# Two more groups of nodes summed from buckets in a graph network's first layer, and self edges only counted there

## The chip, the cores and the metric

The kernel runs on one core of a Trainium2 chip. A core has TensorE (PE; its weight loads are listed as PEld), VectorE (DVE), ScalarE (ACT), GpSimd (POOL) and SyncE (SP), the last of which only issues DMAs here. The metric is the device time of one execution in microseconds. Times of several executions are given by their median.

## The reference

Two layers of a graph network act on 12500 nodes with 128 features each. There are 212500 edges: 100000 drawn at random, the same ones reversed, and one from every node to itself. The list comes sorted by `dst`.

```python
h = relu(layernorm(x))
# layer 0: message passing and a gated cell
msg = h[src] @ W_msg.T + b_msg + edge_embed[type]        # one row per edge
messages = segment_sum(msg, dst)                         # one row per node
x = x + gru_cell(messages, h, W_ih, W_hh, b_ih, b_hh)
# layer 1
h = relu(layernorm(x))
agg = segment_sum(h[dst], src)                           # 'col' is dst, 'row' is src
y = ((1 + eps) * h + agg) @ W1.T + b1
y = relu(batchnorm(y) * gamma + beta)
x = x + y @ W2.T + b2
```

In layer 0 the sum over edges is taken before the matrix: the kernel sums h[src] and counts the edge types of each node, and the small matrices act on these sums.

## The kernel before, in words

**Preparation (to about 123 us).** The rows h are computed, split into three bfloat16 parts that add up to the float32 value (`PARTS0` = 3, so a row has `W0` = 384 columns) and stored in HBM as `table0`. Every edge is packed into one word.

**Two ways of summing in layer 0.** The nodes below `SPLIT0` are summed by *chunks*: a chunk is 128 neighbouring edges of the sorted list. `gather` (L1218) issues one indirect DMA per chunk on POOL's queue, which fetches the 128 source rows from `table0`; eight chunks share a buffer `g`, and there are three such buffers. `match` (L1226) compares the target nodes with a row of places on DVE, eight chunks at once, and L1324 makes a matrix of edge types in the same way. `add_chunk` (L1239, L1242) multiplies each of the three parts with the match and adds one matmul that counts the types; where a chunk crosses a border of 256 nodes, each of these is cut in two.

The nodes from `SPLIT0` on are summed by *buckets*. The last 7056 nodes form 28 groups of 252 nodes, and the first `FIRST` groups of them go by chunks. A bucket holds the edges from one block of 256 source nodes to one group of targets, at most 128. All of `table0` lies in SBUF for it, as `held`. For each of the `NB` = 49 blocks, `take_rows` (L1377) selects up to 128 rows by two matmuls with a 0/1 matrix `take`, ACT turns the result into bfloat16 `rows` (L1379), and `put_rows` adds them to the group's sums by three matmuls (L1386) with a 0/1 matrix `put`, and to the type counts by a fourth (L1388). `put_rows` runs two buckets behind `take_rows`. `prepare` builds `take`, `put` and `kind` for four buckets (`UNIT`) at a time on DVE (L1358, L1363, L1369) and loads the source numbers `others` on SP's queue (L1354).

Edges from a node to itself have an extra place: with every node having at least one, they would overfill the bucket that holds the node's own block. So each group has three more buckets (`PORTIONS` = 3, `NV` = 52), one for each third of the group's nodes. Before, their rows are taken from `held` as well, at a place that L948 to L961 work out edge by edge when the buckets are sorted (L922 to L928 make the offsets). Their type code is raised by 9, so that the counts of types 9 to 17 are those of self edges.

**The sort.** `make_buckets` sorts the words of each group on DVE by a sorting network (L476), with transposes on TensorE, and writes the lists back; up to about 373 us a step of it follows every chunk. `make_list` sorts the list for layer 1 in the same manner, later, beside the loop. Its end makes a row of numbers on POOL (`starts`, L350), which DVE needs (L351).

**The loop and its order.** One loop runs over the chunks. Once the buckets are made, the loop issues, after each chunk, as many bucket steps and list steps as keep them in proportion to the chunks that are left, so that chunks, buckets and the list end together. While the buckets are made, the order of the instructions on each engine is the one that is written; afterwards it is planned ahead by a scheduler.

**The cell.** When 512 nodes (504 in the bucket stream) are summed, a `cell` is queued: a generator whose steps are issued one after every second chunk. It multiplies the sums and the type counts with the small matrices (L635, L636), reads off how many self edges each node has (L643, `times`, which scales the node's own row in layer 1), turns the node's own rows into columns (`hT`, L653, L656), computes the gates (L661 to L664), the new row (L669 to L688), its layernorm, and stores rows for layer 1. Every one of these steps uses the same PSUM bank, `work`. The sums `own` and the counts `types` may be written again for the next 512 nodes once `sl.consumed` is set.

**Layer 1 (from about 1600 us).** It has chunks (gathers from `front1`) and buckets (`back1`) of its own. Its first bucket loads wait until the space of `held` is free. The groups of `back1` that are written last are loaded late; which these are depends on `FIRST` (`late_`).

Of the kernel before, what the change touches and what calls it, by code (L numbers as in the profile page):

```python
# [38 lines left out]
F32 = mybir.dt.float32  # L39
# [12 lines left out]
P = 128  # L52
# [12 lines left out]
FRACTION = 10  # L65
FIRST = 10
SUB = 256
# [10 lines left out]
def tile_gnn(  # L78
# [45 lines left out]
    PORTION = -(-GROUP // PORTIONS)  # L124
    TOP_TILE = 2 * NB - 2
    assert D == P and EC <= FULL and E <= P * FULL and N < NPAD and E % P
# [194 lines left out]
    for h in range(2):  # L321
# [298 lines left out]

    def cell(sl, own, types, pool, psum, store):

# [4 lines left out]
        def work():  # L627
            return psum.tile([P, SLICE], F32, name="work")
# [3 lines left out]
        xs = load_x(sl, pool)  # L632
        yield
        pm = work()
        nc.tensor.matmul(pm[:, :n], env.w["msg"][:, 0, :], own[:, :n], start=True, stop=False)  # L635
# [12 lines left out]
        sl.consumed = True  # L648
        yield
        tp = work()  # L650
        for k, r_ in tiles:
            for j in range(PARTS0):
                nc.tensor.matmul(tp[:, k * high:k * high + r_], hp[:r_, k, j * D:(j + 1) * D],  # L653
                                 ident16[:r_, :r_], start=j == 0, stop=j == PARTS0 - 1)
        hT = pool.tile([D, SLICE], F32, name="hT")
        nc.scalar.copy(hT[:, :n], tp[:, :n])  # L656
        yield
# [249 lines left out]
    def make_buckets(keys, pool, psum):  # L907
# [13 lines left out]
        for k in range(PORTIONS):  # L921
            nc.vector.tensor_scalar(tile_i[:, k, :], lead, float(k * PORTION), None, op0=OP.add)  # L922
        nc.vector.tensor_single_scalar(tile_i, tile_i, P.bit_length() - 1, op=OP.logical_shift_right)
        nc.vector.tensor_scalar(more, tile_i, float(TOP_TILE), float(-P), op0=OP.min, op1=OP.mult)
        for k in range(PORTIONS - 1, 0, -1):
            nc.vector.tensor_tensor(more[:, k, :], more[:, k, :], more[:, k - 1, :], op=OP.subtract)
        nc.vector.tensor_scalar(more[:, 1:, :], more[:, 1:, :], float(BLOCK), None, op0=OP.add)
        nc.vector.scalar_tensor_tensor(more[:, 0, :], more[:, 0, :], float(NB * BLOCK), lead, op0=OP.add,  # L928
                                       op1=OP.add)
        yield from wait(2)  # L930
# [10 lines left out]
        for c in range(0, HALF, some):  # L941
            h = c // some
            word = raw[:, c:c + some]
            here, over = scratch[:, :some], scratch[:, some:]
            ints = [part.tile([P, some], I32, name=f"ints{k}") for k in range(3)]
# [309 lines left out]
    with tc.tile_pool(name="cell", bufs=1) as pool, tc.tile_pool(  # L1255
# [5 lines left out]
        class Stream:  # L1261
# [83 lines left out]
        def bucket_steps():  # L1345
# [4 lines left out]
            def prepare(g, b0):  # L1350

                others = unit.tile([P, UNIT * P], BF16, name="others")
                a = sources0[g, b0:b0 + UNIT, :]
                nc.sync.dma_start(others, bass.AP(tensor=a.tensor, offset=a.offset,  # L1354
                                                  ap=[[0, P], [1, UNIT * P]]))
                i, j = divmod(b0, QJ)
# [11 lines left out]
                for t in range(2):  # L1368
                    nc.vector.tensor_scalar(take[:, t, :], others, own_row[:, 2 * t:2 * t + 1], None,  # L1369
                                            op0=OP.is_equal)  # L1370
                return take, put, kind

            def take_rows(g, b, take):
                t0 = 2 * b if b < NB else min((SPLIT + g * GROUP + (b - NB) * PORTION) // P, TOP_TILE)
                ps = next(taken_banks)[:, :W0]
                for t in range(2):
                    nc.tensor.matmul(ps, take[:, t, :], held[:, t0 + t, :], start=t == 0, stop=t == 1)  # L1377
# [4 lines left out]
            def put_rows(h, rows_, put, kind):  # L1382
                sums, counts = by_bucket.sums.of(h)
                final = by_bucket.sums.used(h)
                for j in range(PARTS0):
                    nc.tensor.matmul(sums[:, :GROUP], rows_[:, j * D:(j + 1) * D], put, start=False,  # L1386
                                     stop=final and j == PARTS0 - 1, skip_group_check=True)
                nc.tensor.matmul(counts[:, :GROUP], kind, put, start=False, stop=final,  # L1388
                                 skip_group_check=True)
                by_bucket.sums.flush()  # L1390
# [4 lines left out]
            for u, (g, b0) in enumerate(units):  # L1395
                take, put, kind = coming
                for k in range(UNIT):
                    rows_ = take_rows(g, b0 + k, take[:, :, k * P:(k + 1) * P])
                    flying.append((g - FIRST, rows_, put[:, k, :], kind[:, k, :]))
                    if len(flying) > LAG:  # L1400
# [404 lines left out]
```

## Time and profile before

| | us |
|---|---|
| median of the three runs shown | 2594.92 (2593.8 to 2598.58) |
| the profiled execution, its own time | 2603.78 |
| its span, from the first to the last instruction | 2602.0 |
| TensorE busy (modelled) | 2250.3 (86%) |
| weight loads busy | 1896.3 (73%) |
| VectorE busy | 2117.8 (81%) |
| ScalarE busy | 1322.5 (51%) |
| GpSimd busy | 1860.4 (71%) |
| gathers of layer 0 (L1218 from `table0`) | 1064, 1006 ns each |
| count matmuls of buckets (L1388) | 936 |

How to read the rows: a line of a group or of the timeline names the line of the kernel, the engine, the operation, what is written and what is read, the shapes and how often. "MATMUL bank<-put,rows 128*128 128x252" has 128 x 128 weights and 252 columns that pass through them. In the timeline, neighbouring instructions of one kind are merged: the first number is the start of the first, the second the time to the end of the last. A matmul's end is modelled, and matmuls overlap; the distance from one start to the next is what a matmul costs when TensorE is never idle. A float32 matmul appears as two instructions. In the rows of waits, the releaser is the engine whose work came last; "issue" means that nothing was waited for that the profile shows. The granted clock (PEclk) is the share of full speed that TensorE was allowed. Indirect DMAs are POOL's instructions, and their busy time is the time that POOL needs to issue them.

### The profile page before, as it was taken

The numbers are of one execution on the slowest core, as the hardware profiler recorded it, in microseconds if no ns is written. First come the engines' busy times: TensorE is split into PE (matmuls) and PEld (weight loads), VectorE is DVE, ScalarE is ACT, GpSimd is POOL, SyncE is SP. The second block draws the span as 40 slices with busy tenths as digits, with TensorE's granted clock in tenths as the row PEclk, the third lists the DMA queues.
The fourth block names the chain that finished last, engine by engine and source line by source line (L and its number), as shares of the span: only waits on it lengthen the run. The fifth ranks groups of instructions, "written<-read, shape, count | busy, mean of one in ns | idle before, by whom it ended". The sixth has DMA issues, their size and how long they took to land. (4 is left out here: it accounts for less than half of the span.)

```text
span 2602.0 us, 52858 instructions
## 1 busy us (share of the span) xinstructions
PE 2250.3 (86%) x19810; PEld 1896.3 (73%) x19834; DVE 2117.8 (81%) x3899; ACT 1322.5 (51%) x2726; POOL 1860.4 (71%) x1886
## 2 busy tenths in 40 slices
PE   2033469899999999999999797899999999999996
PEld 1023347677677777777777575799999999999995
DVE  8898759896568878788787565699999999999983
ACT  4475125455566655656565364444444444444443
POOL 4876477777777777777777676377777777777770
PEclk9996659999999999999999898899999999999998
DMA  5662234454445444545455356655555555555584
GB/s 155 203 205 67 84 100 128 122 128 127 131 132 143 131 134 127 149 129 132 127 150 131 90 144 187 171 154 156 157 158 159 159 159 156 159 160 160 153 217 128
DMA packets 308267, 374.73 MB, mean 144 GB/s; under 512 B 44815, under 2 KB 263093, under 8 KB 308001
## 3 DMA queue, kind: packets, MB, share of 16 engines
q0 software_dynamic: 85504, 197.27, 28.7%
q1 hardware_dynamic: 217451, 171.44, 23.3%
q8 instruction: 158, 2.59, 0.4%
q10 hardware_dynamic: 5046, 2.55, 0.3%
q14 instruction: 108, 0.88, 0.1%
HBM read 327.18 MB, written 43.91 MB: 143 GB/s over the span
## 5 line engine op out<-in xcount | busy, mean ns | idle before, releaser
L1218 POOL DMA_INDIRECT g<-table,idx x1064 | 1070.9, 1006 | 354.9 <-issue 298.4
L1218 POOL DMA_INDIRECT g<-front,idx x690 | 692.8, 1004 | 258.5 <-issue 189.5
L1239 PE MATMUL bank<-m,g 128*128 128x128 bf16 (+25 forms) x5790 | 687.8, 232 | 101.5 <-DMA g<-table,idx 53.0
L1379 ACT CAST rows<-bank 128x384 bf16<-128x384 f32 x936 | 441.8, 478 | 410.3 <-PE bank L1377 407.6
L1542 ACT CAST rows<-bank 128x512 fp32r<-128x512 f32 x686 | 402.7, 588 | 470.8 <-PE bank L1539 468.3
L1539 PE MATMUL bank<-mine,take 126*128 126x256 f32 x2744 | 475.0, 295 | 16.0 <-issue 11.6
L1377 PE MATMUL bank<-held,take 128*128 128x384 bf16 x1872 | 464.5, 328 | 2.4 <-ACT rows L1379 1.6
L1386 PE MATMUL bank<-put,rows 128*128 128x252 bf16 x2808 | 460.1, 272 | 0.0
L1239 PEld LDWEIGHTS <-g 128*128 128x128 bf16 x3912 | 299.5, 103 | 200.0 <-DMA g<-table,idx 94.5
L1552 PE MATMUL bank<-put,rows 128*128 128x256 f32 x2744 | 443.1, 284 | 2.2 <-DVE put L1527 1.9
L1527 DVE TENSOR_TENSOR put<-places,nodes 128x1024 fp32r<-128x1024 f32 x343 | 412.9, 1213 | 5.4 <-PE bank L1552 5.4
L1358 DVE TENSOR_TENSOR put<-places,nodes 128x1008 bf16<-128x1008 f32 x234 | 281.3, 1202 | 157.0 <-PE bank L1388 156.7
L1539 PEld LDWEIGHTS bank<-mine,take 126*128 126x128 f32 x2744 | 374.2, 191 | 28.0 <-issue 21.8
L1552 PEld LDWEIGHTS bank<-put,rows 128*128 128x128 f32 x2744 | 378.0, 190 | 6.8 <-issue 3.6
L1386 PEld LDWEIGHTS <-rows 128*128 128x128 bf16 x2808 | 274.9, 98 | 130.1 <-issue 4.1
L1522 DVE TENSOR_SCALAR take<-others,own_row 126x512 fp32r<-126x512 bf16 x686 | 302.4, 491 | 64.1 <-PE bank L1539 33.6
L1226 DVE TENSOR_TENSOR m<-places,to 128x1024 bf16<-128x1024 f32 (+1 forms) x220 | 312.4, 1420 | 20.3 <-PE bank L1242 11.9
L476 DVE TENSOR_TENSOR key<-key 128x512 f32<-128x512 f32 (+1 forms) x470 | 297.2, 666 | 12.0 <-ACT key L607 4.0
L1239 PEld LDWEIGHTS bank<-m,g 128*128 128x128 f32 x1878 | 270.9, 190 | 2.7 <-DMA g<-front,idx 1.6
L1242 PE MATMUL bank<-m,kindsc 128*128 128x128 bf16 (+2 forms) x1304 | 269.9, 218 | 0.0
L1388 PE MATMUL bank<-put,kindsb 128*128 128x252 bf16 x936 | 254.4, 272 | 0.0
L1369 DVE TENSOR_SCALAR take<-others,own_row 128x512 bf16<-128x512 bf16 x468 | 151.6, 360 | 38.9 <-PE bank L1377 38.4
(329 smaller groups left out, 2189.7 us busy)
## 6 DMA issues: line engine op xcount, KB each, us to landing
others<-sources SPq DMA_DIRECT2D x343, 126.0 KB
others<-sources SPq DMA_DIRECT2D x234, 128.0 KB
g<-table,idx POOLq DMA_INDIRECT x1064
g<-front,idx POOLq DMA_INDIRECT x690
xs<-in_x_dram SPq DMA_DIRECT2D x39, 256.0 KB
table<-hp SPq DMA_DIRECT2D x24, 384.0 KB
held<-table SPq DMA_DIRECT2D x24, 384.0 KB
mine<-back SPq DMA_DIRECT2D x28, 252.0 KB
```

The lines of the kernel that those rows point to most:

```text
L476: nc.vector.tensor_tensor(o, a, b, op=op)
L1218: nc.gpsimd.indirect_dma_start(out=into if table is table0 else into.bitcast(F32), out_offset=None, in_=table, in_offset=bass.IndirectOffs ...
L1226: nc.vector.tensor_tensor(m[:, :n, :], places[:, None, :w].to_broadcast([P, n, w]), to[:, c0:c0 + n, None].to_broadcast([P, n, w]), op=OP. ...
L1239: nc.tensor.matmul(tiles[0][:, lo:hi], g[:, j * D:(j + 1) * D], mk, start=False, stop=final and j == parts - 1, skip_group_check=True)
L1377: nc.tensor.matmul(ps, take[:, t, :], held[:, t0 + t, :], start=t == 0, stop=t == 1)
L1379: nc.scalar.copy(rows_, ps)
L1386: nc.tensor.matmul(sums[:, :GROUP], rows_[:, j * D:(j + 1) * D], put, start=False, stop=final and j == PARTS0 - 1, skip_group_check=True)
L1522: nc.vector.tensor_scalar(take[:GT, t, :n * P], others[:GT, :n * P], own_row[:GT, t:t + 1], None, op0=OP.is_equal)
L1527: nc.vector.tensor_tensor(put[:, :n, :], places[:, None, :].to_broadcast([P, n, BLOCK]), nodes1[:, j, q:q + n, None].to_broadcast([P, n, B ...
L1539: nc.tensor.matmul(ps[:, k, :], take[:GT, t, :], mine[bucket[1]][:GT, t, :], start=t == 0, stop=t == 1)
L1542: nc.scalar.copy(rows_, ps)
L1552: nc.tensor.matmul(to[:, c:c + BLOCK], rows_[:, k, j * D:(j + 1) * D], put, start=False, stop=final and j == PARTS - 1, skip_group_check=True)
```

## The change

`FIRST` becomes 8: 20 groups instead of 18 are summed from buckets, and the chunks cover 7460 instead of 7964 nodes. In the three self-edge buckets of each group the rows are neither taken nor put; only their types are counted. So the sums of the bucket stream lack the self edges, and the cell of that stream adds them: a matmul with `all_self` (a row of ones where the type is a self type, in all 128 columns) writes the number of self edges of each node to all 128 partitions, and two DVE instructions multiply it with `hT` and add it to `own`. For that, the transposes of the node's own rows move ahead of the message. In `make_buckets`, the place of a self edge is now only the number of its portion, so the offsets and some instructions per edge word go. A unit with one real bucket loads and compares only a quarter of the source numbers.

```diff
-FIRST = 10
+FIRST = 8
...
+    all_self = const.tile([NC, P], F32, name="all_self")
     own_self = const.tile([NC, 1], F32, name="own_self")
     nc.vector.tensor_scalar(own_self, own_row[:NC, 0:1], float(NTYPES), None, op0=OP.is_ge)
+    nc.vector.tensor_copy(all_self, own_self[:, 0:1].to_broadcast([NC, P]))
...
-    def cell(sl, own, types, pool, psum, store):
+    def cell(sl, own, types, pool, psum, store, add_self=False):
...
         xs = load_x(sl, pool)
         yield
+        tp = work()
+        for k, r_ in tiles:
+            for j in range(PARTS0):
+                nc.tensor.matmul(tp[:, k * high:k * high + r_], hp[:r_, k, j * D:(j + 1) * D],
+                                 ident16[:r_, :r_], start=j == 0, stop=j == PARTS0 - 1)
+        hT = pool.tile([D, SLICE], F32, name="hT")
+        nc.scalar.copy(hT[:, :n], tp[:, :n])
+        yield
+        if add_self:
+            ps = work()
+            nc.tensor.matmul(ps[:, :n], all_self, types[:, :n], start=True, stop=True)
+            again = pool.tile([D, SLICE], F32, name="gate0")
+            nc.vector.tensor_mul(again[:, :n], hT[:, :n], ps[:, :n])
+            nc.vector.tensor_add(own[:, :n], own[:, :n], again[:, :n])
+            yield
         pm = work()
...
         sl.consumed = True
-        yield
-        tp = work()
...
-        hT = pool.tile([D, SLICE], F32, name="hT")
-        nc.scalar.copy(hT[:, :n], tp[:, :n])
         yield
...
-        tile_i = pool.tile([P, PORTIONS, 2], I32, name="tile_i")
-        more = pool.tile([P, PORTIONS, 2], F32, name="more")
...
-            nc.vector.tensor_scalar(here, there, more[:, 0, h:h + 1], None, op0=OP.add)
-            for k in range(1, PORTIONS):
-                nc.vector.tensor_scalar(over, there, float(k * PORTION), more[:, k, h:h + 1],
-                                        op0=OP.is_ge, op1=OP.mult)
-                nc.vector.tensor_tensor(ints[0] if k == PORTIONS - 1 else here, here, over, op=OP.add)
+            nc.vector.tensor_scalar(here, there, float(PORTION), None, op0=OP.is_ge)
+            for k in range(2, PORTIONS):
+                nc.vector.scalar_tensor_tensor(here, there, float(k * PORTION), here, op0=OP.is_ge, op1=OP.add)
+            nc.vector.tensor_scalar(ints[0], here, float(BLOCK), float(NB * BLOCK), op0=OP.mult, op1=OP.add)
...
-                    queue.add(cell(sl, self.own, self.types, pool, turnp, store_fast))
+                    queue.add(cell(sl, self.own, self.types, pool, turnp, store_fast, not self.apart))
...
+                n = min(UNIT, NB - b0)
                 others = unit.tile([P, UNIT * P], BF16, name="others")
-                a = sources0[g, b0:b0 + UNIT, :]
+                a = sources0[g, b0:b0 + n, :]
...
-                    nc.vector.tensor_scalar(take[:, t, :], others, own_row[:, 2 * t:2 * t + 1], None,
-                                            op0=OP.is_equal)
+                    nc.vector.tensor_scalar(take[:, t, :n * P], others[:, :n * P], own_row[:, 2 * t:2 * t + 1],
+                                            None, op0=OP.is_equal)
...
-            def take_rows(g, b, take):
-                t0 = 2 * b if b < NB else min((SPLIT + g * GROUP + (b - NB) * PORTION) // P, TOP_TILE)
+            def take_rows(b, take):
...
-                for j in range(PARTS0):
+                for j in range(PARTS0 if b < NB else 0):
...
-                    rows_ = take_rows(g, b0 + k, take[:, :, k * P:(k + 1) * P])
+                    b = b0 + k
+                    rows_ = take_rows(b, take[:, :, k * P:(k + 1) * P]) if b < NB else None
```

More of the change, by code (lines that the diff above doesn't have):

```diff
@@ L124, in tile_gnn @@
     PORTION = -(-GROUP // PORTIONS)
-    TOP_TILE = 2 * NB - 2
     assert D == P and EC <= FULL and E <= P * FULL and N < NPAD and E % P
@@ L648, in cell @@
         sl.consumed = True
-        yield
-        tp = work()
-        for k, r_ in tiles:
-            for j in range(PARTS0):
-                nc.tensor.matmul(tp[:, k * high:k * high + r_], hp[:r_, k, j * D:(j + 1) * D],
-                                 ident16[:r_, :r_], start=j == 0, stop=j == PARTS0 - 1)
-        hT = pool.tile([D, SLICE], F32, name="hT")
-        nc.scalar.copy(hT[:, :n], tp[:, :n])
         yield
@@ L915, in make_buckets @@
         nc.vector.tensor_scalar(lead, own_group, float(GROUP), float(SPLIT), op0=OP.mult, op1=OP.add)
-        tile_i = pool.tile([P, PORTIONS, 2], I32, name="tile_i")
-        more = pool.tile([P, PORTIONS, 2], F32, name="more")
[L921 to L929, printed above, removed]
         yield from wait(2)
@@ L943, in make_buckets @@
             word = raw[:, c:c + some]
-            here, over = scratch[:, :some], scratch[:, some:]
+            here = scratch[:, :some]
             ints = [part.tile([P, some], I32, name=f"ints{k}") for k in range(3)]
@@ L1350, in prepare @@
             def prepare(g, b0):
+                n = min(UNIT, NB - b0)
                 others = unit.tile([P, UNIT * P], BF16, name="others")
-                a = sources0[g, b0:b0 + UNIT, :]
-                nc.sync.dma_start(others, bass.AP(tensor=a.tensor, offset=a.offset,
-                                                  ap=[[0, P], [1, UNIT * P]]))
+                a = sources0[g, b0:b0 + n, :]
+                nc.sync.dma_start(others[:, :n * P], bass.AP(tensor=a.tensor, offset=a.offset,
+                                                             ap=[[0, P], [1, n * P]]))
                 i, j = divmod(b0, QJ)
@@ L1368, in prepare @@
                 for t in range(2):
-                    nc.vector.tensor_scalar(take[:, t, :], others, own_row[:, 2 * t:2 * t + 1], None,
-                                            op0=OP.is_equal)
+                    nc.vector.tensor_scalar(take[:, t, :n * P], others[:, :n * P], own_row[:, 2 * t:2 * t + 1],
+                                            None, op0=OP.is_equal)
                 return take, put, kind
-            def take_rows(g, b, take):
-                t0 = 2 * b if b < NB else min((SPLIT + g * GROUP + (b - NB) * PORTION) // P, TOP_TILE)
+            def take_rows(b, take):
                 ps = next(taken_banks)[:, :W0]
                 for t in range(2):
-                    nc.tensor.matmul(ps, take[:, t, :], held[:, t0 + t, :], start=t == 0, stop=t == 1)
+                    nc.tensor.matmul(ps, take[:, t, :], held[:, 2 * b + t, :], start=t == 0, stop=t == 1)
                 rows_ = taken.tile([P, W0], BF16, name="rows")
@@ L1380, in take_rows, with put_rows @@
                 return rows_
-            def put_rows(h, rows_, put, kind):
+            def put_rows(h, b, rows_, put, kind):
                 sums, counts = by_bucket.sums.of(h)
                 final = by_bucket.sums.used(h)
-                for j in range(PARTS0):
+                for j in range(PARTS0 if b < NB else 0):
                     nc.tensor.matmul(sums[:, :GROUP], rows_[:, j * D:(j + 1) * D], put, start=False,
-                                     stop=final and j == PARTS0 - 1, skip_group_check=True)
+                                     stop=b == NB - 1 and j == PARTS0 - 1, skip_group_check=True)
                 nc.tensor.matmul(counts[:, :GROUP], kind, put, start=False, stop=final,
@@ L1397, in bucket_steps @@
                 for k in range(UNIT):
-                    rows_ = take_rows(g, b0 + k, take[:, :, k * P:(k + 1) * P])
-                    flying.append((g - FIRST, rows_, put[:, k, :], kind[:, k, :]))
+                    b = b0 + k
+                    rows_ = take_rows(b, take[:, :, k * P:(k + 1) * P]) if b < NB else None
+                    flying.append((g - FIRST, b, rows_, put[:, k, :], kind[:, k, :]))
                     if len(flying) > LAG:
```

## The prediction

> **What bounds the kernel now.** I read the busy times by stage first, then the waits by stage, then the timeline of TensorE, because a busy share of TensorE is modelled. Only the layer-0 loop and the sort in front of it are touched; layer 1 (from 1600 us on) keeps its work.
>
> Busy microseconds of each engine by stage; in brackets instructions; then granted clock, DMA share, GB/s:
>
> ```profile
> core 0: us, PE busy (x) PEld busy (x) DVE busy (x) ACT busy (x) POOL busy (x), PEclk, DMA share, GB/s
> 123.00:373.00 250.00, 103.58 (x862) 77.16 (x862) 197.63 (x362) 100.75 (x266) 166.90 (x169) 0.73 0.41 120
> 373.00:700.00 327.00, 308.33 (x2856) 231.01 (x2856) 265.46 (x526) 177.45 (x381) 252.39 (x245) 0.96 0.48 127
> 700.00:1460.00 760.00, 751.90 (x7236) 569.62 (x7235) 587.84 (x1225) 459.04 (x997) 581.50 (x583) 1.00 0.51 134
> 1460.00:1500.00 40.00, 23.65 (x180) 16.60 (x179) 20.98 (x51) 11.08 (x22) 24.19 (x26) 0.79 0.29 70
> ```
>
> Up to 373 us the sort builds the buckets while 150 of the 1064 chunks pass (the gathers of L1218 in the window 123 to 373). From 373 to 1600 us, 1227 us, the other 914 chunks and all 936 buckets run together. In this loop two engines compete. POOL issues a gather every 1.30 us (760 us for 583), 1.00 us of it busy and 0.30 us "issue". TensorE must be judged by distances between starts:
>
> ```profile
> 1008.73 0.33 PE L1239 MATMUL bank<-m,g 128*128 128x128 bf16 x3
> 1008.89 0.22 PE L1242 MATMUL bank<-m,kindsc 128*128 128x128 bf16 x1
> 1008.95 0.49 PE L1377 MATMUL bank<-held,take 128*128 128x384 bf16 x2
> 1009.27 0.49 PE L1386 MATMUL bank<-put,rows 128*128 128x252 bf16 x3
> 1009.60 0.27 PE L1388 MATMUL bank<-put,kindsb 128*128 128x252 bf16 x1
> 1009.70 1.02 PE L635 MATMUL work<-ownc,w_msg 128*128 128x512 f32 x2
> 1010.66 1.12 PE L636 MATMUL work<-typesc,emb 18*128 18x512 f32 x2
> 1011.71 0.34 PE L1239 MATMUL bank<-m,g 128*128 128x128 bf16 x3
> ```
>
> From start to start: a chunk takes 0.22 us (1008.73 to 1008.95), a bucket 0.32 for its two takes, 0.33 for its three sums and 0.10 for its count, 0.75 together; a float32 matmul with 512 columns, which is two instructions, 0.96 to 1.05 us. A chunk cut by a 256-node border takes 0.29 us (1004.41 to 1004.70); 1304 count matmuls on 1064 chunks mean 240 cut ones, so the mean is (824 x 0.22 + 240 x 0.29) / 1064 = 0.236 us. In 700 to 1460 us there are 595 buckets (count matmuls of L1388), 583 chunks, 14 cells (28 halves of L635) of about 10 us each (its matmuls' distances, L635 to L700, added up) and 116 sort transposes of 0.11 us: 446 + 138 + 143 + 13 = 740 of 760 us. So TensorE bounds this stage. The waits say the same, stage by stage (us in total, times, longest): 373 to 700, then twice 700 to 1460, then 1460 to 1500:
>
> ```profile
> PE bank L1239 <- DMA g<-table,idx: 12.6, 8, 2.8
> ```
> ```profile
> PE bank L1239 <- DMA g<-table,idx: 0.2, 1, 0.2
> ```
> ```profile
> POOL g L1218 <- issue: 161.8, 531, 0.3
> ```
> ```profile
> PE work L676 <- DVE new L672: 16.1, 1, 16.1
> ```
>
> Before 700 us TensorE still waits for gathers, and POOL sets the pace (245 gathers in 327 us, 1.33 each). After it TensorE waits for none (0.2 us), while POOL keeps going, its idle time nearly all "issue". The two are almost in balance. At 1468 us TensorE stands still for 16.1 us: DVE waits 16.3 us for the iota of L350, which is queued on POOL behind gathers.
>
> **The change, part by part.** TensorE, in the loop:
> - 67 chunks fewer (1064 to 997, from the formula of CH0 with FIRST = 8): -67 x 0.236 = -15.8 us.
> - Buckets: 18 groups x 52 = 936 now. After: 20 x 52 = 1040, but the last three of each group keep only their count, so takes and sums run 20 x 49 = 980 times. That is +44 x (0.32 + 0.33) = +28.6 us and +104 x 0.10 to 0.11 = +11 us.
> - Self edges of the bucket stream come back in the cell, through one more float32 matmul (all_self by types, 504 columns). L636 has the same shape of work, 1.05 us. Only the bucket stream does it, 10 cells: +10.5 us.
> - Cells stay 25 (16 + 9 now, 15 + 10 after).
> Sum: +34.3 us of TensorE, spread evenly over the loop, since the loop paces buckets by chunks.
>
> What comes off, by stage:
> - POOL loses 67 gathers of 1.30 us, 87 us. It has 847 left in the loop, about 1100 us, and is no longer a bound. The 12.6 us of gather waits up to 700 us can go. They don't all go: TensorE's work there is its share, 245 of 914, of 1141 + 34 us (1141: 936 x 0.75, 914 x 0.236, 21 cells x 10, the transposes), 315 us for what are then 227 chunks, 1.39 per chunk against POOL's 1.33, so POOL's lead builds up slowly. I take 9 of 12.6. After such waits the granted clock falls: from 508.33 to 513.87 us the same matmuls stand twice as far apart (0.64 instead of 0.32), 2.5 us lost; it happens again after 680 us. I take 4 us for both.
> - The stall at 1468 us: POOL is some gathers behind there. With slack it would be nearer, but the iota still queues behind a batch of eight gathers (10 us) at most. Between 0 and 16 us come back; I take the middle, 8.
> - The sort, 123 to 373 us: DVE is 98% busy up to 225 us, so its instructions count. The five of L957 to L961 take 3.11 us per half (127.77 to 130.88); three remain, two like L959 (0.49) and one like L954 (0.72), 1.7 us. Twice 1.4 is 2.8 us. The nine small ones of L922 to L928 add up to 5.5 us around 112 to 116 us; there POOL's split of the rows ends last (119 us and after), so between 0 and 5 come back; I take 1. Together -4 us.
>
> What lies beside: 26 more preparations on DVE (put 1.20, kind 0.22, two takes 0.36: 2.1 us each, 56 us), with 20 of the units taking only a quarter of the width, 8 match units fewer (1.5 us each) and two additions of 0.69 us in 10 cells: about +50 us on 936 us busy of 1227 (76%). DVE waits 157 us for TensorE at L1358 in the loop, so this is covered; uncovered it would be the 50 us. ACT gets 44 casts of 0.48 us, 21 us on 708 busy of 1227. SP gets 26 more loads, 20 of the units a quarter as wide. The cell's transposes of hp move ahead of the message. The load of hp is issued right after the last cell's transposes (1017.58 us after 1016.72) and used at 1061, so two steps earlier it still lands long before. The moved copies to PSUM and the new product use the one work bank: 10 times a wait for DVE of 0 to 0.7 us, the worst of L686's; I take 2 us in all. The last bucket cell, after 1600 us, becomes about 3 us longer, beside layer 1's first matmuls; 0 to 3, I take 0.
>
> Sum: +34.3 - 9 - 4 - 8 - 4 + 2 = **+11 us** with the middle values; with all credits in full (12.6, 5, 16, 8) -7, with none +36. The profiled execution took 2603.78 us (span 2602.0); the median of the runs shown is 2594.92, 9 us lower. I put the difference on the median: 2594.9 + 11 = **2606 us**.
>
> A rule speaks against this. The Trainium skill, "Perfetto Trace Analysis", section "Identifying the Most-Contended Engine", says that matmul busy time is no good measure of TensorE's headroom and that the share of weight loading is. By the rule (PEld 569.62 of 760, 75%) TensorE would have a quarter of the stage free, the added matmuls would vanish in it, and POOL's 87 us would come off, about 2508 us. The distances between starts in this trace leave 20 of 760 us, so I don't follow it here.
>
> **Rivals.**
> - Faster by the waits: the credits come in full. POOL's lead makes the iota free (16 us), the gather waits and the low clock go (18), the sort gives 8, and TensorE's 34 us are outweighed by 42 to 45. It decides from the point at which POOL runs a whole batch ahead all the time; for it speaks that POOL's work falls 7% in the loop; against it that the iota stays in POOL's queue. Price: -7 us, some small waits more, 2580 to 2590.
> - POOL the true bound of all stages: then 40 to 88 us come off, 2507 to 2555. For it: POOL never waits long for TensorE from 700 to 1460 us. Against it: TensorE waits 0.2 us for gathers there.
> - Slower by new waits: no stall is shortened, and DVE, 4% busier, or the one work bank delays TensorE. Then +34 to +50: 2629 to 2645.
> - Nothing to see: credits a little above my middle cancel the 34 us: 2590 to 2600.
>
> **How the numbers follow.** Forecast, TensorE-bound with part of the credits, +6 to +28 (2601 to 2623): 0.46. Nothing to see: 0.20. Credits in full: 0.17. POOL the bound: 0.05. New waits: 0.12. The bound for a change that can be told is 0.2%, 5.2 us, 2589.7 to 2600.1. Faster: 0.17 + 0.05 = 0.22; same: 0.20; slower: 0.46 + 0.12 = 0.58. The range leaves out POOL the bound, the lower edge of the full credits and most of the new waits: 2583 to 2630; the forecast's own is 2601 to 2623.
>
> **What would show it.** In the changed profile: 997 gathers at L1218; the loop with almost no wait of TensorE for gathers; POOL with long waits for bank, because TensorE frees buffers late; the stage from 373 us 4 to 24 us longer; starts as far apart as now. The stall on the iota should be shorter than 16 us. The forecast is wrong if the loop gets shorter than 1220 us, or if TensorE shows waits for take, put or work that aren't there now.

## The result, and the profile after

The changed kernel takes 2611.88 us (median of 4 runs, 2611.51 to 2615.43). The kernel before, run beside it, takes 2596.09 us (4 runs, 2593.8 to 2598.58). The ratio is 1.0065 with a 95% interval from 1.0053 to 1.0078: slower by 15.8 us, three times the 0.2% from which the prediction calls a change one that can be told. The forecast was 2606 us, in a range from 2583 to 2630.

The profiled execution of the changed kernel took 2615.43 us (span 2613.6), 3.6 us above its median; that of the kernel before took 2603.78 us, 7.7 us above the median of 2596.09. So the two traces differ by 11.65 us where the medians differ by 15.8. Both differences are used below, each under its name.

For the experiments e1 to e4 and e9 to e12 the chip was in a condition in which the kernel before itself took 3551 and 3553 us, with TensorE interrupted again and again, so that each of their ratios counts only against the kernel before in the same condition.

Busy times by stage in the trace after (the stage and its length, then PE, PEld, DVE, ACT and POOL in us with the instructions in brackets; then granted clock, DMA share, GB/s):

```profile
123.00:373.00 250.00, 104.19 (x870) 78.22 (x870) 192.79 (x352) 101.50 (x267) 163.14 (x167) 0.72 0.40 117
373.00:700.00 327.00, 318.60 (x2871) 235.37 (x2871) 277.76 (x557) 183.09 (x397) 239.28 (x233) 0.98 0.48 126
700.00:1460.00 760.00, 750.38 (x7033) 564.75 (x7031) 602.93 (x1266) 456.71 (x994) 532.13 (x531) 1.00 0.49 127
1460.00:1500.00 40.00, 38.28 (x333) 27.76 (x330) 30.00 (x67) 22.17 (x46) 26.47 (x28) 1.00 0.36 92
```

TensorE is now busy in 1460 to 1500 us too (38.28 us instead of 23.65, clock 1.00 instead of 0.79), and the clock before 700 us is 0.98 instead of 0.96. POOL issues 531 gathers in the long stage where it issued 583. The waits of TensorE in the loop (385 to 1600 us), the longest three, and then those of POOL from 700 to 1460 us:

```profile
PE work L694 <- DVE hT L690: 4.6, 10, 0.8
PE work L708 <- ACT gate L702: 3.5, 10, 1.1
PE work L651 <- DVE ownb L648: 2.1, 4, 0.8
```
```profile
POOL g L1212 <- issue: 143.2, 470, 0.3
POOL g L1212 <- PE bank L1236: 60.3, 21, 5.8
POOL g L1212 <- PE bank L1233: 15.1, 9, 3.5
```

No row of TensorE waiting for a gather is left, and the stop of 16.1 us on `new` is gone. It is POOL that waits now, 75 us in 30 waits, for TensorE to free a buffer of chunks. TensorE's timeline after, at about the same place:

```profile
1006.71 0.33 PE L1233 MATMUL bank<-m,g 128*128 128x128 bf16 x3
1006.88 0.22 PE L1236 MATMUL bank<-m,kindsc 128*128 128x128 bf16 x1
1006.94 0.33 PE L1233 MATMUL bank<-m,g 128*128 128x128 bf16 x3
...
1012.60 0.49 PE L1371 MATMUL bank<-held,take 128*128 128x384 bf16 x2
1012.93 0.48 PE L1380 MATMUL bank<-put,rows 128*128 128x252 bf16 x3
1013.25 0.27 PE L1382 MATMUL bank<-put,kindsb 128*128 128x252 bf16 x1
...
1014.20 1.11 PE L645 MATMUL work<-typesb,all_self 18*128 18x504 f32 x2
1015.24 0.50 PE L1371 MATMUL bank<-held,take 128*128 128x384 bf16 x2
```

The starts are as far apart as before: 0.23 us for a chunk, 0.33 + 0.32 + 0.10 for a bucket. The new matmul of the self edges, L645, takes 1.04 us to the next start.

**Where the 11.65 us of the traces came from.** The work can be marked by its first and last take on TensorE:

| | before | after | difference |
|---|---|---|---|
| start to the first take | 377.75 | 384.74 | +7.0 |
| first to last take of layer 0 | 1221.6 | 1224.6 | +3.0 |
| last take to the first of layer 1 | 30.8 | 32.6 | +1.7 |
| from there to the end | 971.75 | 971.71 | 0.0 |

Inside the loop I added up TensorE's distances from start to start. For each shape of matmul the lower quartile of its distances stands for the undisturbed one; what exceeds it is a stop (over 0.4 us or behind an idle time), a stretch of slowed starts, or small change. How the shapes are grouped moves the first row by 1 to 2 us.

| us | before | after | e6, self edges only counted |
|---|---|---|---|
| undisturbed work | 1134.2 | 1163.2 | 1106.9 |
| stops: gathers | 14.3 | 0 | 35.2 |
| stops: the list's iota | 17.4 | 0 | 17.2 |
| other stops | 19.5 | 23.4 | 21.7 |
| slowed starts and small change | 36.3 | 38.1 | 38.2 |
| loop | 1221.6 | 1224.6 | 1219.0 |

TensorE got 29.0 us more of undisturbed work, 27.8 us less of stops and 1.8 us more of slowed starts.

### The profile page after: what moved, and what is told of

The parts are those of the page before. It is cut to its first block, busy times and chain, and to the rows that moved or that the text cites. A ratio compares the mean times of both kernels' runs of the same rounds, so it can differ in the third digit from the quotient of the medians.

```text
span 2613.6 us, 53062 instructions
## 1 busy us (share of the span) xinstructions
PE 2283.0 (87%) x19821; PEld 1913.5 (73%) x19844; DVE 2159.2 (83%) x3995; ACT 1339.5 (51%) x2768; POOL 1789.7 (68%) x1819
## 3 DMA queue, kind: packets, MB, share of 16 engines
q0 software_dynamic: 82288, 190.68, 27.8%
## 5 line engine op out<-in xcount | busy, mean ns | idle before, releaser
L1212 POOL DMA_INDIRECT g<-table,idx x997 | 1004.8, 1008 | 432.3 <-issue 273.1
L1233 PE MATMUL bank<-m,g 128*128 128x128 bf16 (+26 forms) x5541 | 664.1, 234 | 88.2 <-DMA g<-table,idx 60.9
L1373 ACT CAST rows<-bank 128x384 bf16<-128x384 f32 x980 | 460.3, 477 | 390.2 <-PE bank L1371 386.1
L1380 PE MATMUL bank<-put,rows 128*128 128x252 bf16 x2940 | 479.2, 272 | 0.5 <-DVE put L1353 0.3
L1353 DVE TENSOR_TENSOR put<-places,nodes 128x1008 bf16<-128x1008 f32 x260 | 312.1, 1201 | 133.4 <-PE bank L1382 133.0
L1233 PEld LDWEIGHTS <-g 128*128 128x128 bf16 x3663 | 277.9, 103 | 188.0 <-issue 90.0
L1220 DVE TENSOR_TENSOR m<-places,to 128x1024 bf16<-128x1024 f32 (+2 forms) x212 | 302.1, 1426 | 14.7 <-PE bank L1233 6.5
L1382 PE MATMUL bank<-put,kindsb 128*128 128x252 bf16 x1040 | 281.6, 272 | 0.0
L1236 PE MATMUL bank<-m,kindsc 128*128 128x128 bf16 (+8 forms) x1221 | 253.5, 219 | 0.0
L1364 DVE TENSOR_SCALAR take<-others,own_row 128x512 bf16<-128x512 bf16 (+1 forms) x520 | 167.0, 356 | 65.4 <-PE bank L1371 42.1
```

The costliest lines, as they stand in the source:

```text
L1212: nc.gpsimd.indirect_dma_start(out=into if table is table0 else into.bitcast(F32), out_offset=None, in_=table, in_offset=bass.IndirectOffs ...
L1220: nc.vector.tensor_tensor(m[:, :n, :], places[:, None, :w].to_broadcast([P, n, w]), to[:, c0:c0 + n, None].to_broadcast([P, n, w]), op=OP. ...
L1233: nc.tensor.matmul(tiles[0][:, lo:hi], g[:, j * D:(j + 1) * D], mk, start=False, stop=final and j == parts - 1, skip_group_check=True)
L1353: nc.vector.tensor_tensor(put, places[:, None, :GROUP].to_broadcast([P, UNIT, GROUP]), nodes0[:, j:j + UNIT, i, g - FIRST:g - FIRST + 1].t ...
```

## The experiments

The order is by question, not by time. In the expectations T is the theory of the forecast (TensorE bounds the loop, and the sum of its matmuls with the credits sets the time).

### Which engine bounds the kernel before?

**e5_fewer_gathers_2** (e4 is the same kernel). 66 gathers of layer 0 are left out; the chunk concerned is summed from the rows of the chunk before it. TensorE keeps all its matmuls.

```diff
+            if table is table0 and k == BATCH - 1 and c0 // BATCH % 2:
+                continue
...
-                add_chunk(first_chunks, c, g[:, k, :], m[:, k, :], by_chunk.sums, tm[:, k, :])
+                of = k - 1 if k == BATCH - 1 and c0 // BATCH % 2 else k
+                add_chunk(first_chunks, c, g[:, of, :], m[:, k, :], by_chunk.sums, tm[:, k, :])
```

> The run with 66 gathers left out once more (rows of the chunk before it are used instead), because the first one fell on a chip on which the kernel before takes 3551 us. On a chip where it takes about 2596: theory T (TensorE bounds the loop): 10 to 35 us less than before, 2561 to 2586. Rival R1 (POOL bounds it): 86 us less, about 2510.

Measured: 2563.1 us against 2594.62, ratio 0.9873 [0.9859, 0.9888], -32 us. POOL's 66 gathers of 1.30 us are 86 us, so most of what POOL gave up brought nothing. POOL's waits from 700 to 1460 us show where it went:

```profile
POOL g L1220 <- issue: 147.5, 484, 0.3
POOL g L1220 <- PE bank L1244: 34.6, 15, 10.3
POOL g L1220 <- PE bank L1241: 9.8, 6, 3.8
```

POOL waits for TensorE, as in the changed kernel. The trace's undisturbed work of TensorE is that of before, 1134.2 us; the 23.5 us that its loop is shorter (1198.1) are, up to rounding, stops on gathers (14.3 to 0), on the iota (17.4 to 9.1) and 2.7 us of slowed starts, with 1.9 us more of other stops. Another 6.2 us of the 29.5 us between the two traces lie in layer 1, which the edit doesn't touch; their cause isn't shown.

So with 66 gathers fewer TensorE bounds the loop. In the kernel before, POOL has no room either: between the first and the last take it is busy for 929 us and stands 280 us in gaps of 0.3 us next to its gathers, 1209 of 1221.6 us. TensorE's undisturbed work, slowed starts and other stops are 1190 us; the rest are the 31.7 us of stops on gathers and on the iota. Neither engine bounds that kernel alone; how much the relief of TensorE brings is seen in e6.

**e4_fewer_gathers**, the same in the interrupted condition:

> The kernel before with 66 of its 1064 gathers left out: the last chunk of every second batch of eight uses the rows fetched for the chunk before it, so the sums are of other rows; matmuls, matches and their order stay. T: POOL's relief alone brings only what TensorE waits for, gathers 12 to 14 us, the low clock after them 4 to 5, and of the stall on the iota 8 to 16: 10 to 35 us less, 2561 to 2586. R1: 66 gathers of 1.30 us, 86 us less, 2505 to 2515. If the early part (sort up to 373 us) is held by gathers too, as the transposes queue behind chunks on TensorE, up to 10 us more come off there.

Measured: 3491.22 us against 3551.05, ratio 0.9831 [0.9785, 0.9876]. It says nothing that e5 doesn't, because TensorE's interruptions (waits on "issue" alone are 178 us of its loop) move with everything else.

### The two halves of the change

**e6_self_only_2** (e1 is the same kernel): the change with 18 groups. An unused copy is left out to make room.

```diff
-FIRST = 8
+FIRST = 10
...
-    places16 = lists.tile([P, BLOCK], BF16, name="places16")
-    nc.scalar.copy(places16, places)
```

> The changed kernel with FIRST back at 10, once more. T: TensorE loses 25.7 us in the loop but POOL keeps 914 gathers in it, so POOL becomes the bound and 5 to 20 us come off: 2576 to 2591. R1: no change, 2593 to 2599. R2 (new waits of the rearranged cell): 2600 or more.

Measured: 2607.74 us against 2594.62, ratio 1.0052 [1.0039, 1.0065], +13 us. My theory had it faster and fell here. The work left TensorE as computed, 1134.2 to 1106.9 us, and the time stayed. TensorE's waits in its loop, and the long stage of the windows:

```profile
PE bank L1231 <- DMA g<-table,idx: 30.0, 31, 2.5
PE work L684 <- DVE new L680: 17.0, 1, 17.0
```
```profile
700.00:1460.00 760.00, 733.34 (x7006) 550.30 (x7005) 586.84 (x1228) 435.58 (x949) 583.15 (x581) 0.99 0.50 132
```

POOL issues 581 gathers in the stage, two fewer than before: its pace did not change. In the loop it is busy for 929 us and stands 278 us in gaps of 0.3 us, 1207 of 1219 us, as in the kernel before, and TensorE's stops on gathers are 35 us instead of 14. So with 18 groups POOL sets the pace: 27 us less work on TensorE shortens the loop of the trace by 2.6 us. That explains 0, not +13: the span of this trace (2601.5) is that of the trace before (2602.0), but the trace is the shortest execution of e6 (2603.41) and that of before lies high. What the ordinary executions of e6 lose is not to be seen in it and stays open.

**e1_self_only**, the same in the interrupted condition:

> The changed kernel with FIRST back at 10: only the second half of the change, self edges counted and not summed in the buckets, with 18 groups and 1064 chunks as before. (An unused copy of the places, L764 of before, is left out to make room.) Theory T (TensorE bounds the loop, POOL follows closely, waits on gathers and on the iota come on top): TensorE loses 54 takes and sums of 0.65 us, 35 us, and gains nine self matmuls of 1.05 us, 25.7 us less in all; but POOL keeps 914 gathers in the loop, at least 1190 us, so it becomes the bound and only 5 to 20 us come off: 2576 to 2591 us, ratio 0.993 to 0.998, with gather waits of TensorE above 20 us in the loop. Rival R1 (POOL is the true bound now): no change, 2593 to 2599. Rival R2 (the loss comes from new waits of the rearranged cell): slower than before, 2600 or more.

Measured: 3535.56 us, ratio 0.9932 [0.9899, 0.9965], 0.7% lower, where e6 is slower. That would fit: POOL's gathers are as fast as ever (1.30 us) and TensorE is slowed, so POOL waits 559 of the loop's 1748 us for TensorE to free its buffers, and TensorE's saving can count. But in that condition the kernel before, run against itself, reads 0.35% low (e9), so little of the 0.7% is sure.

**e2_first8_only**: the kernel before with `FIRST = 8`, self edges kept in the buckets.

```diff
-FIRST = 10
+FIRST = 8
```

> The kernel before with FIRST = 8 and nothing else: 20 groups from buckets, self edges summed in them as before. T: TensorE gets 104 whole buckets of 0.755 us and loses 67 chunks of 0.236 us, +62.7 us, less the 26 us of waits that the changed kernel lost in its loop: +33 to +42 us, 2629 to 2638 us, ratio about 1.014. R1: POOL's 67 gathers come off, 2510 to 2560. R2: about as before, 2590 to 2600, because the cell isn't rearranged.

Measured: 3598.12 us, ratio 1.0113 [1.0071, 1.0155], +47 us. By the prediction's prices this is 104 x 0.75 - 15.8 = +62 us of TensorE. The sign and the order are right; the condition of the chip forbids more.

**e3_no_add**: the changed kernel without the matmul, the product and the addition of the self edges in the cell, so that the sums of the bucket stream lack them.

```diff
-        if add_self:
-            ps = work()
-            nc.tensor.matmul(ps[:, :n], all_self, types[:, :n], start=True, stop=True)
...
-            nc.vector.tensor_add(own[:, :n], own[:, :n], again[:, :n])
-            yield
```

> The changed kernel without the matmul with all_self, the product and the addition: the self edges of the bucket stream are left out of the sums. T: ten float32 matmuls of 1.05 us go from a loop that TensorE bounds, so 9 to 12 us come off the changed kernel's 2611.9: 2600 to 2603, ratio to the kernel before about 1.002. R1: 0, 2611 to 2613. R2 (its waits on the one work bank and on DVE are the loss): 16 us or more come off, 2596 or less.

Measured: 3561.74 us, ratio 1.0027 [0.9995, 1.0059]: no different from the kernel before. The changed kernel itself wasn't run in this condition, so the expectation, which is a difference to it, stays untested. What the addition costs can be read only in the changed kernel's own trace: 1.04 us per cell of TensorE, and 2.8 us of stops on `ownb` in all.

### The stop on the iota, and the preparation

In the kernel before, two small iotas stand on POOL behind gathers: that of the list's starts (the stop of 16.1 us) and `edge_of`, which the sort needs. **e8_before_iotas** makes both early:

```diff
+    starts(some_chunks, to1, epool, "from_i1")
...
+        edge_of = iota(pool, [P, NV], [[-BLOCK, NV]], base=-BLOCK, name="edge_of")
+        nc.vector.tensor_scalar(edge_of, edge_of, 0.5, None, op0=OP.add)
...
-        starts(some_chunks, to1, keys, "key")
```

> The kernel before with the same two iotas moved ahead. T: the stop of 16.1 us at 1468 us and the low clock after it go, 14 to 19 us; edge_of brings 0 to 1, as the words are ready only then: 2577 to 2583. Rival: the time is given back, because POOL is the bound and its gathers are late anyway: 2590 to 2596.

Measured: 2588.69 us against 2594.62, ratio 0.9975 [0.9965, 0.9986], -6 us, where 12 to 18 were expected. Of the versions run undisturbed it is the only one that beats the kernel before without leaving work out. What is left in its trace of the wait on `new` is this:

```profile
PE work L677 <- DVE new L673: 1.1, 1, 1.1
```

The loop is 1202.7 us, 18.9 shorter than in the trace before, but the medians differ by 6. A good part of the 16 us may be peculiar to the one execution that was profiled, which also lies 7.7 us above its median. That isn't shown: e6's trace, the shortest of its executions, has a stop of 17.0 us there too, and e5's one of 7.7 us. A small part is given back at the start, where the sort begins at 148.70 us instead of 146.03 and the first take comes 2.1 us later. How long the stop usually is, these runs don't say.

**e7_after_iotas** does the same to the changed kernel:

> The changed kernel with two iotas moved ahead: edge_of, which DVE waits 6.1 us for in front of the sorting network in the changed kernel's trace (146.7 us), is made before the first gather, and the list's starts (L350 of before) in the preparation. T, which puts the missing 4 us of the sort on that wait: the network starts up to 6 us earlier and 3 to 6 us come off the changed kernel; the starts bring nothing there, since its stall on them is gone (TensorE's longest stop is 1.4 us): 2606 to 2609. If the sort is held by the gathers instead: 0, 2611 to 2613.

Measured: 2610.33 us against 2594.62, ratio 1.0056 [1.0044, 1.0068], 1.5 us below the changed kernel's 2611.88: no difference that can be told. The changed kernel waits for `edge_of`. DVE's timeline of the changed kernel:

```profile
120.42 0.43 DVE L943 TENSOR_SCALAR ints<-key 128x512 int32<-128x512 int32 x1
...
140.04 0.49 DVE L965 TENSOR_SCALAR key<-key,factor 128x512 f32<-128x512 f32 x1
146.64 0.19 DVE L969 TENSOR_SCALAR edge_of<-edge_of 128x52 f32<-128x52 f32 x1 [6.11 <-POOL edge_of L279]
```

DVE begins the words at 120.42 us (124.02 before), needs 20.1 us for them instead of 22.0, is done at 140.5 (146.0 before), and then stands 6.11 us until POOL has come past its gathers to the iota. The sort begins at 146.74 us where it began at 146.03. Why the words begin earlier is seen on POOL, here after:

```profile
117.06 1.05 POOL L918 DMA_INDIRECT key<-packed,row_edge  x1 [0.16 <-issue]
...
121.90 0.99 POOL L448 TENSOR_TENSOR hp<-h,hp 128x256 bf16<-128x256 f32 x1
125.83 1.04 POOL L1212 DMA_INDIRECT g<-table,idx  x1 [2.94 <-DMA table<-hp]
```

The gathers of the raw words (L918) have moved ahead of POOL's last splits of the node rows (L445 to L448). So the splits end at 122.89 us, and the gathers of the chunks, which wait for the table, begin at 125.83 us, not at 123.36 as before. This comes with `FIRST` = 8 and hardly with the shorter preparation. e2, which changes `FIRST` alone, has the late table too; its first gather of a chunk on POOL, and its wait for the iota on DVE:

```profile
126.24 1.12 POOL L1218 DMA_INDIRECT g<-table,idx  x1 [2.87 <-DMA table<-hp]
```
```profile
147.54 0.19 DVE L975 TENSOR_SCALAR edge_of<-edge_of 128x52 f32<-128x52 f32 x1 [4.85 <-POOL edge_of L280]
```

(The interrupted condition makes no difference so early: the sort begins at 146.12 us in e9 and at 146.03 in the trace before.) In e6, which has the shorter preparation alone, the chunks' gathers begin at 123.74 us, DVE waits 2.46 us for the iota, and the sort begins at 144.40 us; its last matmuls (L1015 of before) begin at 309.40 us, 1.8 us earlier than the 311.24 of before.

In e7 the raw words are gathered behind the splits again (120.58 us, the splits end at 119.96), and the chunks' gathers begin at 123.33. But its iota stands behind the raw words on POOL, at 122.90 us, and DVE waits for it there:

```profile
123.13 0.19 DVE L926 TENSOR_SCALAR edge_of<-edge_of 128x52 f32<-128x52 f32 x1 [5.80 <-POOL edge_of L279]
```

The words begin only at 126.48 us, and the sort at 145.93. So the edit moved the wait ahead of the words and didn't take it away; the first take comes 1.6 us earlier (383.16). What the sort would gain without the wait isn't shown.

### Transposes ahead of the message

**e9_before_again** is the kernel before, unchanged, to see how far its trace and time repeat.

> The kernel before, unchanged, profiled once more, to see how much of its first trace is that one execution's: its own time there, 2603.78, lies above all other executions of it (2591 to 2600). Ratio 1.000 within 0.0015. If the stop on the list's starts is as long in it as before (16 us), then hoisting the starts (which brought 5.9 us) gave back two thirds of it elsewhere; if it is 4 to 8 us, hoisting brought just the stop, and my credit of 8 us was taken from an unusual execution.

Measured in the interrupted condition: 3543.36 us against 3552.51, ratio 0.9965 [0.9941, 0.9988]. It is the same kernel, and yet the interval leaves out 1, so differences below some 0.6% there mean nothing. The length of the stop couldn't be learnt in this condition.

**e10_moved_only** is the kernel before with the transposes of `hp` ahead of the message in every cell.

```diff
         yield
+        tp = work()
...
+        nc.scalar.copy(hT[:, :n], tp[:, :n])
+        yield
         pm = work()
...
-        tp = work()
...
-        nc.scalar.copy(hT[:, :n], tp[:, :n])
-        yield
```

> The kernel before with one part of the change: in every cell the transposes of hp stand ahead of the message. Theory T3: this order alone makes the loop start later, because the load of the next hp, which waits for these transposes, now stands ahead of the first loads of others on SP's queue; 2 to 5 us, 2597 to 2600, and the first take on TensorE 2 to 5 us later than in the kernel before. Rival R2: it is the whole of what the self-edge half costs (13.1 us): 2605 to 2610. Rival: nothing, 2593 to 2596.

Measured: 3588.98 us, ratio 1.0094 [1.0061, 1.0127]. That is slower by 36 us, beyond the 0.6%. The traces of e10 and e9 differ by 72 us: 50 of these lie in layer 1 (1364.9 against 1314.9 us), which the edit doesn't touch, and 23.6 in the loop (1773.2 against 1749.6). So how much of the ratio is the move's can't be told. One thing repeats what the changed kernel shows. On SP the next load of `hp` now stands ahead of the first loads of `others`; in the trace before, and after:

```profile
358.66 30.08 SPq L1354 DMA_DIRECT2D others<-sources  x7
390.63 0.33 SPq L210 DMA_DIRECT2D hp<-table  x1
```
```profile
371.87 0.31 SPq L209 DMA_DIRECT2D hp<-table  x1
373.12 5.59 SPq L1349 DMA_DIRECT2D others<-sources  x4
```

`hp` waits there for the first cell's transposes to have read its buffer, and `others` waits behind it: 14.5 us later than before. DVE stands 11.48 us for `others`, and its first instruction that builds a `take` comes at 377.00 us instead of 361.99. In e10 it comes 14 us later too (414.47 against 400.38 in e9). But TensorE's first take comes only 7.0 us later in the changed kernel, and 1.6 us earlier in e10, since it has other work until then. From the begin of the sort's last matmuls to the first take on TensorE pass 65.0 to 66.8 us in the undisturbed traces with the transposes in their old place (e5, before, e8) and 70.5 to 71.1 in those with the transposes ahead (e7, the changed kernel, e6): the move goes with some 4 us more, with 18 groups too.

**e12_after_iotas_order** is e7 with the transposes ahead only in the cells of the bucket stream, where the self edges need them; **e11_self_iotas_order** is the same with 18 groups.

```diff
+        if add_self:
+            hT = turn_rows()
+            yield
...
+        if not add_self:
+            hT = turn_rows()
+            yield
```

> The changed kernel (FIRST = 8) with the iotas moved ahead and the transposes ahead only in the bucket stream's cells. TensorE bounds this loop. T3: the loop starts 2 to 5 us earlier: 2605 to 2608 against 2610.3 with the iotas alone. R2: 2595 to 2600. Nothing: 2609 to 2612.

> The self-edge half at FIRST = 10, with the two iotas moved ahead and with the transposes ahead of the message only in the cells that need them so (the bucket stream). POOL bounds this loop (907 gathers of 1.32 us, 98% of it). T3: the order brings 2 to 5 us and the starts 6 us, as they did on the kernel before: 2597 to 2600. R2: if the order is the 13 us, 2586 to 2591.

Measured: e12 3563.48 us, ratio 0.9995 [0.9959, 1.0031]; e11 3526.84 us, ratio 0.9905 [0.9865, 0.9945]. e11 stands with e1 (0.9932): in this condition the takes and sums saved seem to pay. With the same kernel reading 0.9965, no more can be drawn from the times. The traces do show that the order is the cause of the late `others`: where it is kept out of the other stream's cells, DVE's first `take` comes at 401.46 us in e12 and 398.03 in e11, without a wait, as in e9. What the order alone costs in an undisturbed run was not settled.

## Why the prediction was right in sign, and where its terms were off

- **TensorE bounds the loop: right for the changed kernel, half right for the kernel before.** In the changed kernel POOL waits 122 us of the loop for TensorE, and no stop on a gather is left. In the kernel before POOL was full as well (1209 of 1221.6 us). The prediction has the numbers, 583 gathers at 1.30 us, which fill 758 of the stage's 760 us, but it judged by TensorE's 740 of 760 us alone. e5 shows that 86 us off POOL brought 32; e6 shows that 27 us off TensorE brought 2.6 us of loop. The sum holds all the same, because it starts from TensorE's whole loop and takes off its stops on POOL.
- **The rule that the prediction didn't follow.** The Trainium skill, "Perfetto Trace Analysis", section "Identifying the Most-Contended Engine", names the weight loading's share as a measure of TensorE's headroom, with the share of peak FLOPs beside it, which the prediction left out. By the weight loading's share the prediction's estimate was about 2508 us; it was 2611.88. The distances between starts decide here.
- **+34.3 us of TensorE: 29.0 measured** (1134.2 to 1163.2). The self matmul was 1.05 us by its neighbour and is 1.04.
- **Gather waits -9 and the clock -4: -14.3 and almost nothing.** All of the gather waits went, not the larger part. I had let POOL's lead build up slowly, at 1.39 us a chunk against 1.33; but from 373 to 700 us POOL already waits 19 us for buffers of chunks (it issues 233 gathers there, 245 before), so it had its lead from the start of the loop. The granted clock rose by 0.02 from 373 to 700 us, but the slowed starts of the loop didn't shrink (36.3 to 38.1 us with the small change).
- **The iota -8: -17.4 in the traces.** With POOL ahead of TensorE, DVE got the iota in time (POOL made it at 1489.21, and TensorE's longest stop in the loop is 1.4 us). In ordinary executions the term may be smaller: e8 removed the stop and gained 6 us.
- **The sort -4: this step failed, it is +7.0 before the first take.** I counted DVE's instructions, which became fewer by 1.9 us and began 3.6 us earlier, 5.5 us where I had 4, and took it that their end starts the sort. The next instruction waits for a POOL iota that is queued behind gathers. So the 5.5 us turned into 6.11 us of waiting, and the sort begins 0.7 us later than before. Two things came in between. `FIRST` = 8 moves the raw words' gathers ahead of the last splits in POOL's queue (e2 has it too), so the table was written later, the chunks' gathers began 2.5 us later, and the sort's last matmuls begin at 313.97 us instead of 311.24: 2.7 of the 7.0 us. With 18 groups (e6) the shorter preparation did bring 1.8 us of the 4. The other 4.3 us lie between the sort and the first take. The prediction put the moved transposes at nothing, since the load of `hp` would land in time. It left out that the loads of `others` stand behind that load on SP. That these come late by the order is shown (e10, e12); that they make the 4.3 us is argued from the traces with and without it.
- **Hand-over 0: +1.7**, within the 0 to 3 given for the longer last cell. **Work bank +2: 2.8** on `ownb`.
- **Sum: +11 forecast, +11.65 in the traces, +15.8 in the medians.** The first agreement is partly luck: the loop came out at +3.0 where I had +15 (34.3 - 9 - 4 - 8 + 2) and named 4 to 24 as the sign, the start at +7.0 where I had -4. The errors nearly cancel. (With all credits in full the prediction's -7 leaves out its own +2; the sum is -5.) The forecast named "the loop shorter than 1220 us" as what would overthrow it; it is 1224.6 (1221.6 before). Against the medians the loop's credits are too large in the traces, as far as the profiled execution of before was a long one.
- **Rivals.** POOL as the bound of all stages, which would have taken 40 to 88 us off, is out: the changed kernel got slower, and e5 gained 32 us of 86. Of the credits in full, those for gathers and the iota came true in the traces, those for the clock and the sort didn't. New waits: none of size on TensorE in the loop. With 18 groups POOL sets the pace (e6); the two more groups take 67 gathers from it and give the bound to TensorE at +56 us of work (1106.9 to 1163.2). Each half of the change undoes the room that the other makes.

Open: the +13 us of e6 beyond its trace, the usual length of the stop on the iota, what the order of the transposes costs by itself, and why the medians differ by 4 us more than the traces.

## What to carry to other kernels

Where two engines are nearly in balance, price both: work taken from the one comes back as waits for the other, and work moved from the second to the first costs in full. Gaps that stand next to every instruction of an engine are no room. An instruction saved in front of a wait for another engine's queue gains only what that wait leaves, so look for the last thing to arrive; moving a small iota ahead of gathers brought 6 us in one kernel (e8) and only moved the wait in the other (e7). Hold the profiled execution's time against the median before pricing a single stop that it shows.

## Of the hardware, not expected

The same kernel took 3551 us (chip 6, 23 runs) and 3553 us (chip 5, 27 runs) at some times, and 2594.6 us (chip 6, 17 runs) at another. In e9's trace of that condition the granted clock is 0.87 instead of 0.96, and TensorE stands with no releaser that the trace shows; its waits from 450 to 2100 us:

```profile
PE bank L1377 <- issue: 130.7, 80, 4.8
PE bank L1377 <- ACT rows L1379: 89.5, 61, 6.2
PE bank L1239 <- issue: 28.8, 50, 1.2
```

POOL's gathers kept their pace of 1.30 us in it. What interrupts TensorE, these traces don't show.
